# Layers 1 to 3 of the last three pairs batch by batch, turned on TensorE and scaled on VectorE, with closer due dates for the last five pairs

## The chip, the cores and the metric

One core of one Trainium2 chip. The metric is the device time of the whole program in microseconds, as the median of several runs; "span" is the length of the profiled run, some 2 us shorter.

## The reference, cut to what matters

Sixty-four batches of 256 nodes and 128 features pass four layers, each `x = layernorm(x + gnn(x))`. The kernel takes two batches as a pair, so there are 32 pairs (0 to 31), independent of one another.

```
for _ in range(5):                                   # layer 0: five gated steps
    m = adj @ h                                      # used for m_in and m_out
    u3 = h @ u3_w.T + u3_b
    z, r = sigmoid(av @ w3_w.T + w3_b + u3), sigmoid(av @ w4_w.T + w4_b + u3)
    h = (1 - z) * h + z * tanh(av @ w5_w.T + w5_b + (r * h) @ u5_w.T + u5_b)
# layer 1: (A * eye) @ (x W0) + (A * (1 - eye)) @ (x W1) + bias
# layer 2: graph attention (softmax over neighbours), layernorm, relu, GIN, two matmuls
# layer 3: Chebyshev sum over adj, adj^2, adj^3 with seven weight matrices
```

## The kernel before

Every operation is put into a graph with an engine, an estimated cost, and the buffers it touches; a list scheduler then fixes the order on each engine. Among the operations that can start at the same time it takes the lowest rank: the due date of the pair less the longest path from the operation to the pair's end.

```python
def place(p):
    return 20000 * min(p, 28)                        # due date in ns: pairs 28 to 31 are equal
# ...
        for op in reversed(self.ops):
            op.tail = op.cost + max((n.tail + (LATENCY[op.eng] if n.eng != op.eng or op.eng != PE else 0)
                                     for n in op.before), default=0)
        for op in self.ops:
            op.rank = (place(op.rank[0]) - op.tail, op.rank)
```

A "turn" exchanges nodes and features of a tile. VectorE transposes 32x32 blocks, and four DMAs on the SyncE queue put the blocks in place. Layers 1 to 3 have five turns (dT, xT, wT, zT, and xT again), each layer 0 step has one (htok).

```python
        def turn(src, dst, view=lambda b: b.ap, tiles=4):
            S = flat("S") if tiles == 4 else big("S8")
            add(DVE, ..., lambda: nc.vector.transpose(S.ap..., view(src)...), [src], [S], [S])   # cut
            def f():
                for k in range(4):
                    nc.sync.dma_start(dst.ap[:, :, 32 * k:32 * k + 32],
                                      S.ap[32 * k:32 * k + 32].rearrange("s (y r) -> s y r", r=32))
            add(SP, 2730, f, [S], [dst], [dst])
```

The normalisations end with a scaling on ScalarE, in four pieces of 128x128:

```python
                    for c in range(4):
                        nc.scalar.activation(o.ap[:, c, :], view()[:, c, :], AF.Copy, scale=rs.ap[:, c:c + 1])
```

Of the kernel before, what the change touches and what calls it, by code (L numbers as in the profile page):

```python
# [22 lines left out]
N_W = 6  # L23
N_PAIR = 8

MATS = ["w3a", "w3b", "w4a", "w4b", "w5a", "w5b", "u3", "u5",
        "l1w0", "l1w1", "wp", "wpT", "w1", "w2",
        "v0", "v1", "v2", "v3", "v4", "v5", "v6"]
N_L0 = 8
COLS = ["w3_b", "u3_b", "w4_b", "w5_b", "u5_b", "bp", "a_src", "a_dst", "mlp_g", "mlp_b", "e0", "e1"]  # L30
# [8 lines left out]
NORMS = (ACT, ACT, ACT, ACT)  # L39
# [3 lines left out]
def place(p):  # L43

    return 20000 * min(p, 28)
# [111 lines left out]
def kernel(ctx: ExitStack, tc: tile.TileContext, xT, xs, adjs, mats, cols, rows, out):  # L157
# [121 lines left out]
    dg, swap = tall("dg"), tmp([P, P], "swap")  # L279
# [78 lines left out]
    def split():  # L358
        nc.vector.reciprocal(den.ap, den.ap)
        for it in range(2):  # L360
            nc.vector.tensor_scalar(lg.ap[:, it, :], lg.ap[:, it, :], den.ap[:, it:it + 1], None, op0=ALU.mult)
            blk, d = lg.ap[:, it, it * P:(it + 1) * P], dg.ap[:, 0, it * P:(it + 1) * P]
            nc.vector.tensor_mul(d, blk, ident.ap)
            nc.vector.tensor_sub(blk, blk, d)
            nc.vector.tensor_copy(lgs.ap[:, it, :].rearrange("p (t s x) -> p t s x", s=32, x=4),
                                  in_slots(lg.ap[:, it, :]))
        nc.vector.tensor_reduce(dnat.ap, dg.ap[:, 0, :].rearrange("p (t j) -> p t j", j=P), AX.X, ALU.add)
        nc.vector.tensor_copy(swap.ap.rearrange("p (t s x) -> p t s x", s=32, x=4), in_slots(ident.ap))

# [25 lines left out]
    pre(DVE, 2800, split, [ident], [den, lg, dg, lgs, dnat, swap], [dg, lgs, dnat, swap])  # L395
# [75 lines left out]

    t = bank()
# [7 lines left out]

    def build(p):
# [5 lines left out]

        def turn(src, dst, view=lambda b: b.ap, tiles=4):

            S = flat("S") if tiles == 4 else big("S8")  # L490
            add(DVE, 705 if tiles == 4 else 1240,
                lambda: nc.vector.transpose(S.ap.rearrange("p (x c r) -> p x c r", x=4, c=tiles),  # L492
                                            view(src).rearrange("p (c x s) -> p x c s", x=4, c=tiles)),
                [src], [S], [S])

            def f():
                for k in range(4):
                    nc.sync.dma_start(dst.ap[:, :, 32 * k:32 * k + 32],  # L498
                                      S.ap[32 * k:32 * k + 32].rearrange("s (y r) -> s y r", r=32))
            add(SP, 2730, f, [S], [dst], [dst])  # L500
            return dst

        def joined(b):
            return b.ap.rearrange("p t d -> p (t d)")
# [13 lines left out]

        def by_token(terms, consts, also=()):

            t = bank()

            def f():
                for c in range(4):
                    for k, (s, w) in enumerate(terms):
                        nc.tensor.matmul(t.ap[:, c * D:(c + 1) * D], s(c), w,  # L526
                                         start=(k == 0), stop=(k == len(terms) - 1))
            add(PE, 900 * len(terms), f, consts, [t], [t, *also])
            return t

        def full_norm(y):

            st, mv = temp([P, 4, 6], "st", 6), temp([P, 4, 2], "mv", 6)
            rs, nmr = temp([P, 4], "rs", 8), temp([P, 4], "nmr", 6)

            def f():
                for c in range(4):
                    nc.vector.bn_stats(st.ap[:, c, :], y.ap[:, c, :])
                for c in range(4):
                    nc.vector.bn_aggr(mv.ap[:, c, :], st.ap[:, c, :])  # L540
            add(DVE, 1720, f, [y], [st, mv], [st, mv, rs, nmr])

            def f():
                nc.gpsimd.tensor_scalar(rs.ap, mv.ap[:, :, 1], LN_EPS, None, op0=ALU.add)
                nc.gpsimd.tensor_tensor(rs.ap, rs.ap, neg_half.ap, op=ALU.pow)
            add(POOL, 1560, f, [mv, neg_half], [rs])
            add(DVE, 337, lambda: nc.vector.scalar_tensor_tensor(nmr.ap, mv.ap[:, :, 0], -1.0, rs.ap, op0=ALU.mult,
                                                                 op1=ALU.mult), [mv, rs], [nmr])

            def f():  # L550
                for c in range(4):
                    nc.scalar.activation(y.ap[:, c, :], y.ap[:, c, :], AF.Identity, bias=nmr.ap[:, c:c + 1],
                                         scale=rs.ap[:, c:c + 1])
            add(ACT, 1930, f, [nmr, rs], [y])

        def norm(y, view, o, eng, extra=None, takes=()):

            sq, ss, rs = wide("sq"), temp([P, 4], "ss", 6), temp([P, 4], "rs", 8)
            add(ACT, 630, lambda: nc.scalar.activation(sq.ap, view(), AF.Square), [y], [sq], [sq])  # L559

            def f():
                nc.vector.tensor_reduce(ss.ap, sq.ap, AX.X, ALU.add)  # L562
                if extra is not None:
                    nc.vector.scalar_tensor_tensor(ss.ap, ss.ap, 1.0 / D, extra.ap, op0=ALU.mult, op1=ALU.add)  # L564
            add(DVE, 685 if extra is None else 850, f, [sq] + ([] if extra is None else [extra]), [ss], [ss])

            def f():
                if extra is None:
                    nc.gpsimd.tensor_scalar(ss.ap, ss.ap, 1.0 / D, LN_EPS, op0=ALU.mult, op1=ALU.add)  # L569
                nc.gpsimd.tensor_tensor(rs.ap, ss.ap, neg_half.ap, op=ALU.pow)  # L570
            add(POOL, 1400 if extra is None else 1110, f, [ss, neg_half], [ss, rs], [rs])
            if eng == ACT:
                def f():
                    for c in range(4):
                        nc.scalar.activation(o.ap[:, c, :], view()[:, c, :], AF.Copy, scale=rs.ap[:, c:c + 1])
                add(ACT, 1570, f, [y, rs], [o], takes)
            else:
                add(DVE, 700, lambda: nc.vector.tensor_mul(o.ap, view(), rs.ap[:, :, None].to_broadcast([P, 4, D])),
                    [y, rs], [o], takes)
# [6 lines left out]
        for s in range(STEPS):  # L586
# [29 lines left out]
            h = turn(hT, wide("htok"))  # L616
        x_t = h
        add(DVE, 763, lambda: nc.vector.tensor_add(x_t.ap, x_t.ap, x0.ap), [x0], [x_t])
# [5 lines left out]
        def f():  # L624
            for it in range(2):
                o, i = (b.ap.rearrange("p (b t) d -> p b t d", t=2)[:, :, it, :] for b in (xd, x_t))
                nc.scalar.activation(o, i, AF.Copy, scale=dcol.ap[:, it:it + 1])
        add(ACT, 1000, f, [x_t, dcol], [xd], [xd])
        dT = turn(xd, wide("dT"), joined)
        qT = mix(x_t, offT)  # L630
        y = wide("y")
        add(POOL, 1370, lambda: nc.gpsimd.tensor_add(y.ap, x_t.ap, row("l1_bias", 4)), [x_t, rbc], [y], [y])
        t = by_token([(lambda c: qT.ap[:, c * P:(c + 1) * P], mat("l1w1")), (lambda c: dT.ap[:, c, :], mat("l1w0"))],
                     [qT, dT, W1])
        add(DVE, 690, lambda: nc.vector.tensor_add(y.ap, as_tiles(t.ap), y.ap), [t], [y])
        norm(y, lambda: y.ap, y, NORMS[0])
# [3 lines left out]
        xT = turn(x1, wide("xT"), joined)  # L640
        h2 = temp([P, 4, HW], "h2", 6)
        for b in range(2):
            t2 = bank()

            def f(t2=t2, b=b):
                for i in range(2):
                    nc.tensor.matmul(t2.ap[:, i * HW:(i + 1) * HW], xT.ap[:, 2 * b + i, :], wpx.ap,  # L647
                                     start=True, stop=True)
            add(PE, 450, f, [xT, wpx], [t2], [t2] + ([h2] if b == 0 else []))
            add(DVE, 410, lambda t2=t2, b=b: nc.vector.tensor_add(  # L650
                h2.ap[:, 2 * b:2 * b + 2, :], t2.ap[:, :2 * HW].rearrange("p (t d) -> p t d", d=HW),
                hbias.ap[:, None, :].to_broadcast([P, 2, HW])), [t2, hbias], [h2])

        ts, sd = bank(), flat("sd")

        def f():
            for c in range(4):
                nc.tensor.transpose(ts.ap[:, c * P:(c + 1) * P], h2.ap[:, c, D + 1:D + 2].to_broadcast([P, P]), ident.ap)  # L658
        add(PE, 450, f, [h2, ident], [ts], [ts, sd])
        add(ACT, 585, lambda: nc.scalar.copy(sd.ap.rearrange("p (c x s) -> p c x s", x=4, s=32),  # L660
                                             ts.ap.rearrange("p (c s x) -> p c x s", x=4, s=32)), [ts], [sd])
        u = big("u")
        mx, nm, rd = (temp([P, 4], k, 6) for k in ("mx", "nm", "rd"))
# [4 lines left out]
        def f():  # L668
            for c in range(4):
                b, it = divmod(c, 2)  # L670
                nc.vector.tensor_tensor_reduce(
                    out=uc(c), in0=sd.ap[:, b * N:(b + 1) * N], in1=maskb.ap[:, it, :], scale=1.0,
# [4 lines left out]
        add(DVE, 2400, f, [sd, h2, maskb], [u, mx, nm], [u, mx, nm, rd])  # L677

        def f():
            for c in range(4):  # L680
                nc.scalar.activation(uc(c), uc(c), AF.Prelu, bias=h2.ap[:, c, D:D + 1], alpha=SLOPE)
        add(ACT, 2000, f, [h2], [u])

        def f():
            for c in range(4):
                nc.scalar.activation(uc(c), uc(c), AF.Exp, bias=nm.ap[:, c:c + 1], accum_out=rd.ap[:, c:c + 1])
        add(ACT, 2760, f, [nm], [u, rd])
# [124 lines left out]
```

## Time and profile before

| | before |
|---|---|
| median of the first three runs | 1586.88 us (1583.99 to 1587.73) |
| span of the profiled run | 1584.6 us |
| TensorE busy | 1538.7 us, 97% |
| last layer 0 product done | 1462.4 us |
| from there to the end | 122.2 us, with TensorE work of 70.1 |

"TensorE work" here is the number of passes of each width times what a pass takes at full clock, read from start to start where the matmuls are dense: 0.111 us for 128 columns, 0.216 for 256, 0.429 for 512. Over the whole kernel that gives 1515.8 us (some 2 us of it are the few passes of one or two columns in the preparation). Span less work is what is lost: 68.8 us, of which 52.1 (122.2 - 70.1) after the last layer 0 product and 16.7 before it.

### The profile page before, as it was taken

The page shows a single profiled execution, that of the slowest core. Times are in us where ns is not written, and L with a number is a line of the kernel's source. Part 1 is how long each engine was busy: PE and PEld are TensorE (multiplying, and loading weights), DVE is VectorE, ACT ScalarE, POOL GpSimd, SP SyncE. Part 2 cuts the span into 40 slices and gives each one's busy share as a digit, 9 for nine tenths or more (in the row PEclk, how much of TensorE's full clock was granted, in tenths as well). Part 3 has the DMA queues.
Part 4 walks back from the last instruction along what each step waited for, and adds up shares of the span by engine and source line. Part 5 has one row for each costly group of instructions (what it writes and reads, how often), then busy time and mean ns, then how long its engine had stood idle before and what let it go on. Part 6 is the DMA issues. An engine that isn't in the chain of part 4 may idle for free.

```text
span 1584.6 us, 21441 instructions
## 1 busy us (share of the span) xinstructions
PE 1538.7 (97%) x6382; PEld 1070.4 (68%) x6382; DVE 1104.4 (70%) x2465; ACT 992.1 (63%) x2245; POOL 441.5 (28%) x487
## 2 busy tenths in 40 slices
PE   8999999999999999999999999999999999998767
PEld 5556667666677676667676667766767766676656
DVE  4687787667767677767676867776776766677553
ACT  3355676666666666666666666656666666677554
POOL 0001233332222323223323232233232231244441
PEclk9999999999999999999999999999999999999788
DMA  6223444444443444443444444344444344334422
GB/s 204 45 36 52 67 66 84 73 87 84 75 84 74 72 81 87 76 84 74 74 79 87 76 80 79 71 77 87 78 77 85 70 72 88 62 70 68 79 54 60
DMA packets 756611, 121.98 MB, mean 77 GB/s; under 512 B 743184, under 2 KB 743184, under 8 KB 756496
## 3 DMA queue, kind: packets, MB, share of 16 engines
q1 hardware_dynamic: 756208, 120.09, 42.1%
q8 instruction: 52, 0.85, 0.2%
q14 instruction: 63, 0.52, 0.1%
q10 hardware_dynamic: 288, 0.53, 0.1%
HBM read 19.86 MB, written 8.39 MB: 18 GB/s over the span
## 4 chain that ended last, share of the span: by engine, by line
PE 91%; DVE 2%; DMA 2%; ACT 2%; SPq 1%; issue 1%; POOL 1%; POOLq 0%; ACTq 0%; DVEq 0%
PE ps L513 27%; PE ps L607 9%; PE ps L589 9%; PE ps L597 8%; PE ps L605 8%; PE ps L592 8%; PE ps L740 7%; PE ps L526 6%; PE ps L702 4%; PE ps L749 3%; PE ps L647 2%; SPq L498 1%; PE ps L658 1%; DMA wT<-S 1%; DMA hT<-xT_in 1%
## 5 line engine op out<-in xcount | busy, mean ns | idle before, releaser
L516 ACT COPY mix<-ps 128x512 f32<-128x512 f32 x256 | 148.1, 580 | 197.7 <-PE ps L513 196.5
L513 PE MATMUL ps<-aTs,htok 128*128 128x256 f32 x1024 | 242.4, 380 | 2.8 <-DMA htok<-S 2.6
L513 PEld LDWEIGHTS ps<-aTs,htok 128*128 128x128 f32 x1024 | 192.6, 190 | 69.6 <-issue 32.8
L569 POOL TENSOR_SCALAR ss<-ss 128x4 f32<-128x4 f32 x96 | 38.2, 398 | 603.0 <-DVE ss L562 601.7
L611 DVE TENSOR_TENSOR hv<-hv,hT 128x512 f32<-128x512 f32 x160 | 124.2, 777 | 98.8 <-ACT hv L609 97.3
L570 POOL TENSOR_TENSOR rs<-ss,neg_half 128x4 f32<-128x4 f32 x128 | 139.2, 1087 | 192.0 <-DVE ss L564 183.8
L602 DVE SCALAR_TENSOR_TENSOR tr<-tr,hT 128x512 f32<-128x512 f32 x160 | 118.4, 742 | 91.4 <-ACT tr L595 91.3
L607 PE MATMUL ps<-tr,u5h 128*128 128x512 f32 x320 | 163.6, 594 | 0.4 <-DVE tr L602 0.2
L589 PE MATMUL ps<-hT,W 128*128 128x512 f32 x320 | 162.4, 593 | 1.1 <-DMA hT<-xT_in 1.1
L592 PE MATMUL ps<-mix,w4s 128*128 128x512 f32 x320 | 162.9, 593 | 0.0
L597 PE MATMUL ps<-mix,dw 128*128 128x512 f32 x320 | 162.8, 593 | 0.0
L605 PE MATMUL ps<-mix,w5s 128*128 128x512 f32 x320 | 162.6, 593 | 0.0
L609 ACT ACTIVATE hv<-ps,bh 128x512 f32<-128x512 f32 x160 | 109.4, 685 | 83.2 <-PE ps L607 80.6
L600 ACT ACTIVATE tz<-ps,bz 128x512 f32<-128x512 f32 x160 | 109.4, 685 | 60.0 <-PE ps L597 58.6
L595 ACT ACTIVATE tr<-ps,br 128x512 f32<-128x512 f32 x160 | 108.4, 679 | 39.3 <-PE ps L592 39.0
L612 DVE SCALAR_TENSOR_TENSOR hv<-tz,hv 128x512 f32<-128x512 f32 x160 | 108.9, 694 | 24.0 <-ACT tz L600 22.6
L562 DVE TENSOR_REDUCE ss<-sq 128x4 f32<-128x512 f32 x128 | 87.1, 681 | 48.1 <-ACT sq L559 48.1
L492 DVE STREAM_TRANSPOSE S<-hT 128x512 f32<-128x512 f32 x160 | 112.3, 703 | 1.1
L614 DVE SCALAR_TENSOR_TENSOR hT<-hv,hT 128x512 f32<-128x512 f32 x160 | 108.8, 693 | 4.9
L607 PEld LDWEIGHTS ps<-tr,u5h 128*128 128x128 f32 x320 | 60.4, 190 | 50.4 <-issue 36.4
L605 PEld LDWEIGHTS ps<-mix,w5s 128*128 128x128 f32 x320 | 58.6, 191 | 51.5 <-issue 31.1
L589 PEld LDWEIGHTS ps<-hT,W 128*128 128x128 f32 x320 | 58.3, 190 | 49.1 <-issue 42.8
(174 smaller groups left out, 2904.2 us busy)
## 6 DMA issues: line engine op xcount, KB each, us to landing
htok<-S SPq DMA_DIRECT2D x640, 64.0 KB, 2.4
xT<-S SPq DMA_DIRECT2D x256, 64.0 KB, 2.4
wT<-S SPq DMA_DIRECT2D x128, 128.0 KB, 3.8
xs<-xs_in SPq DMA_DIRECT2D x32, 256.0 KB, 2.8
hT<-xT_in SPq DMA_DIRECT2D x32, 256.0 KB, 3.0
dT<-S SPq DMA_DIRECT2D x128, 64.0 KB, 2.3
zT<-S SPq DMA_DIRECT2D x128, 64.0 KB, 2.4
y_out<-o SPq DMA_DIRECT2D x32, 256.0 KB, 2.0
```

The costliest lines, as they stand in the source:

```text
L492: lambda: nc.vector.transpose(S.ap.rearrange("p (x c r) -> p x c r", x=4, c=tiles), view(src).rearrange("p (c x s) -> p x c s", x=4, c=til ...
L513: nc.tensor.matmul(t.ap[:, b * N:(b + 1) * N], src.ap[:, 2 * b + j, :], m.ap[:, j, :], start=(j == 0), stop=(j == 1))
L516: add(ACT, 590, lambda: nc.scalar.copy(o.ap, t.ap), [t], [o])
L570: nc.gpsimd.tensor_tensor(rs.ap, ss.ap, neg_half.ap, op=ALU.pow)
L589: add(PE, 865, lambda tg=tg: nc.tensor.matmul(tg.ap, mat("u3"), hT.ap, start=True, stop=False, skip_group_check=True), [hT, W0], [tg], [tg ...
L592: add(PE, 865, lambda tg=tg, mT=mT: nc.tensor.matmul(tg.ap, w4s.ap, mT.ap, start=False, stop=False, skip_group_check=True), [mT, w4s], [tg])
L597: add(PE, 865, lambda tg=tg, mT=mT: nc.tensor.matmul(tg.ap, dw.ap, mT.ap, start=False, stop=True, skip_group_check=True), [mT, dw], [tg])
L602: add(DVE, 735, lambda tr=tr: nc.vector.scalar_tensor_tensor(tr.ap, tr.ap, 1.0, hT.ap, op0=ALU.add, op1=ALU.mult), [hT], [tr])
L605: add(PE, 865, lambda tv=tv, mT=mT: nc.tensor.matmul(tv.ap, w5s.ap, mT.ap, start=True, stop=False), [mT, w5s], [tv], [tv, hv])
L607: add(PE, 865, lambda tv=tv, tr=tr: nc.tensor.matmul(tv.ap, u5h.ap, tr.ap, start=False, stop=True), [tr, u5h], [tv])
L611: add(DVE, 735, lambda hv=hv: nc.vector.tensor_sub(hv.ap, hv.ap, hT.ap), [hT], [hv])
L740: nc.tensor.matmul(tt[i].ap[:, b * N:(b + 1) * N], s, w.ap.rearrange("p k d -> p (k d)"), start=(b == 0 and k == 0), stop=False, skip_grou ...
```

## The change

The intent is to shorten the end, where TensorE is no longer full. The last three pairs (29 to 31) run layers 1 to 3 as two independent chains of one batch each; in them TensorE transposes through the identity and ScalarE copies the result out of PSUM; VectorE scales; and the due dates of pairs 27 to 31 are 6 us apart in place of 20 us (27 to 28) and none (28 to 31). The five steps of layer 0 stay as they were; the sum and the norm after them already belong to the split chains. Extra copies of some weights in natural order come with it.

```diff
+N_TAIL = 3
 def place(p):
-    return 20000 * min(p, 28)
+    return 20000 * min(p, 27) + 6000 * max(p - 27, 0)
@@ (cut)
+        if p < NPAIR - N_TAIL:
+            layers123(p, add, x_t, x0, (0, 1), False)
+        else:
+            for b in range(2):
+                layers123(p, add, x_t, x0, (b,), True)
+
+    def layers123(p, add, h, x0, bs, by_pe):
+        nb = len(bs)
+        C = 2 * nb
@@ turned(), used for dT, xT, zT and xT of layer 3 (cut)
+            if by_pe:
+                t = bank()
+                def f():
+                    for c in range(C):
+                        nc.tensor.transpose(t.ap[:, c * P:(c + 1) * P], src.ap[:, c, :], ident.ap)
+                add(PE, 112 * C, f, [src, ident], [t], [t, o])
+                ... add(ACT, act(C * P) - 45, lambda: nc.scalar.copy(o.ap, as_tiles(t.ap[:, :C * P])), [t], [o])
+            else:
+                turn(add, src, o, joined)
@@ full_norm (cut)
+            if by_pe:
+                def f():
+                    for c in range(C):
+                        nc.vector.tensor_scalar(y.ap[:, c, :], y.ap[:, c, :], mv.ap[:, c, 0:1], rs.ap[:, c:c + 1],
+                                                op0=ALU.subtract, op1=ALU.mult)
+                add(DVE, 350 * C, f, [mv, rs, nmr], [y])
+                return
@@ norm (cut)
+            if by_pe:
+                add(DVE, dve(C * D), lambda: nc.vector.tensor_mul(o.ap, view(), rs.ap[:, :, None].to_broadcast([P, C, D])),
+                    [y, rs], [o])
+                return
@@ the same for wT; the rest takes C and nb for 4 and 2, and the swapped weights (cut)
```

## The prediction

> **What bounds the kernel now.** I read the page's engine rows and its 40 slices first (is one engine full, and where is it not), then windows over the two halves that differ, then the order of matmuls and TensorE's waits in the part that is not full.
>
> ```profile
> span 1584.6 us, 21441 instructions
> ...
> PE 1538.7 (97%) x6382; PEld 1070.4 (68%) x6382; DVE 1104.4 (70%) x2465; ACT 992.1 (63%) x2245; POOL 441.5 (28%) x487
> ...
> PE   8999999999999999999999999999999999998767
> ...
> PEclk9999999999999999999999999999999999999788
> ```
>
> TensorE is full in 35 slices. The first slice loses 6 us to loads; the last four (some 40 us each) have both idle time and a lower granted clock. So nothing that saves work on another engine helps before about 1420 us.
>
> ```profile
> 400.00:800.00 400.00, 400.00 (x1685) 279.38 (x1684) 289.20 (x642) 260.31 (x595) 115.94 (x128) 1.00 0.44 78
> 1390.00:1430.00 40.00, 40.00 (x197) 30.57 (x195) 30.89 (x86) 30.81 (x74) 19.07 (x21) 1.00 0.39 68
> 1430.00:1463.00 33.00, 29.62 (x151) 22.35 (x150) 24.41 (x61) 22.88 (x59) 11.63 (x15) 1.00 0.48 75
> ...
> 1463.00:1585.00 122.00, 86.69 (x404) 73.85 (x404) 60.00 (x155) 68.43 (x183) 44.46 (x55) 0.84 0.35 63
> ```
>
> Columns: window, length, busy PE, PEld, DVE, ACT, POOL with counts, granted clock, DMA share, GB/s. I cut at 1463 because the timeline has the last layer 0 matmul there; what follows is layers 1 to 3 alone:
>
> ```profile
> 1461.52 1.02 PE L607 MATMUL ps<-tr,u5h 128*128 128x512 f32 x2
> 1462.38 0.60 PE L658 MATMUL ps<-ident,h 128*128 128x128 f32 x4
> 1469.48 3.78 PE L513 MATMUL ps<-aTss,hb 128*128 128x256 f32 x8 [6.50 <-ACT hb L552]
> ```
>
> Full-speed matmul costs, from start to start in the dense timeline: a 512-column product (two passes) 0.86 us, eight 256-column passes 1.73 us, eight 128-column passes 0.89 us. A pair's layer 0 step is 1.73 + 5 x 0.86 = 6.0, five steps 30.2; its layers 1 to 3 are 17.0; together 47.2, times 32 = 1511, plus about 6 of preparation: 1517 us of TensorE work. After 1463 the counts by form are 232 passes of 256 columns and 172 of 128: 232 x 0.216 + 172 x 0.111 = 69 us. In 122 us, then, 53 are lost: 122 - 86.7 = 35 idle, and 86.7 - 69 = 18 to the clock. That is all there is to win, beside some 8 us between 1414 and 1463 and at the start.
>
> What TensorE waits for in that window:
>
> ```profile
> PE ps L513 <- ACT hb L552: 8.6, 2, 6.5
> PE ps L702 <- DMA wT<-S: 7.1, 2, 3.8
> PE ps L513 <- ACT hg L711: 3.7, 1, 3.7
> PE ps L526 <- ACT zT L719: 3.4, 2, 2.0
> PE ps L740 <- DMA xT<-S: 3.2, 2, 2.8
> ```
>
> No single wait dominates: normalisation on ScalarE and GpSimd, and the DMA turns. It is the length of the chain of one pair. The last pair's layers 1 to 3 take from 1463 to the end, 120 us, and four pairs due at the same time (the place function is capped at pair 28) run in lockstep. One turn by DMA in the timeline:
>
> ```profile
> 1520.18 1.25 DVE L492 STREAM_TRANSPOSE S<-u 128x1024 f32<-128x1024 f32 x1
> ...
> 1521.45 3.66 SPq L498 DMA_DIRECT2D wT<-S  x4
> ...
> 1525.21 8.78 SPq L498 DMA_DIRECT2D zT<-S  x12
> ...
> 1527.92 3.33 PE L702 MATMUL ps<-h,wT 128*128 128x128 f32 x16 [3.22 <-DMA wT<-S]
> ```
>
> 7.7 us from the transpose's start to the matmul; and twelve issues for three zT in a row take 8.8 us of one queue, so pairs in lockstep also queue for SyncE.
>
> **What the Trainium skill says.** "TensorE: Matmul & The Clock Gate", Part 4 (PE-mode transpose): a transpose is a matmul against the identity, about 275 ns in a kernel, its result in PSUM, so a copy follows. The trace agrees: the four transposes of L658 last 272 ns each but advance in 0.44 us together, 0.11 each.
>
> ```profile
> 1416.37 0.60 PE L658 MATMUL ps<-ident,h 128*128 128x128 f32 x4
> 1416.81 1.02 PE L597 MATMUL ps<-mix,dw 128*128 128x512 f32 x2
> ```
>
> The same page, Part 1: TensorE falls to half clock after an idle window of about 3.4 us. The trace agrees: after the 6.5 us gap above, the eight passes took 3.6 us to the next group, not 1.73. So a closed gap pays about twice. "DMA: Bandwidth & Descriptors", Anatomy of one DMA: about 2 us of a DMA are fixed, mostly the receipt of the write (its figure is for the GpSimd path). Here, on the SP queue, 64 KB took 2.4 us and 128 KB 3.8, so halving a turn's size alone would have gained little. "SBUF — State Buffer", two separate sides: VectorE with two SBUF inputs and GpSimd lock each other out. In this tail the two-input L725 took 842 ns on average, over the whole kernel 715: it agrees, and the change gives VectorE more of such work.
>
> **The change part by part.** Pairs 29 to 31 become six chains of one batch each.
>
> Removed per such pair: five turns (VectorE 4 x 0.70 + 1.22 = 4.0 us, 20 DMA issues at about 0.65 us, and on the chain four latencies of about 5 us and one of 7.7); on ScalarE the four norm scalings (y, z, o, hg: 4 x 4 x 0.39 = 6.2 us less on the hg, read from PSUM, 0.37), the two full ones (8 x 0.41 = 3.3 us) and the copy sd (0.58).
>
> Added: 24 transposes a pair x 0.11 = 2.7 us of TensorE, 8 us for three pairs. Their copies on ScalarE: an estimate of 0.39 for 256 columns and 0.58 for 512 (from R's 0.37 and mix's 0.58); per batch dT, xT, xT3 and wT make 3 x 0.39 + 0.58 = 1.75, 3.5 us a pair (zT's activation was there before). Scaling on VectorE: 4 x 0.41 per batch (L753's size), and four 128x128 scalings at 0.29 (L411).
>
> VectorE per batch, halves of the measured operations: about 10.7 us (adds and multiplies of 256 columns 0.41 each x 13, statistics 0.6 twice, scores 1.3, u 0.7, the rest small), 21.4 a pair against 18.3 now. ScalarE 9.0 a batch, GpSimd about 7.6 (its pow with two columns instead of four is guessed at 0.65, from 1.01 at four). TensorE 17.0 / 2 + 1.35 = 9.9.
>
> Chain of one batch in layers 1 to 3: I added the same operations in order: today about 92 us for a pair by measured lengths (with the five turns 28), plus 5 of semaphores; the run shows 120 with queueing. For a batch: full norms 2 x 2.7, four norms 9, scores to weights 5.5, turns 5 x 0.7, GpSimd affine 1.5, matmuls 7, copies and adds 8, output 3, semaphores 5: near 48 us.
>
> Due dates: pairs 27 to 31 are now due 6 us apart, where 28 to 31 were equal. With a 48 us chain behind layer 0, the last layer 0 ends with pair 29 some 12 us and pair 30 some 6 us into their layers, and 27 and 28 near their ends: TensorE work left 5 + 7 + 15 + 17 + 20 = 64 us, VectorE 64, ScalarE about 55, GpSimd about 45. No longer the chain (48) but two engines at 64 bound this phase. I take 85% use and a drain of about 5 us: 80 us where 122 are now.
>
> Sum: TensorE work 1517 + 8 + 0.5 = 1525.5, of which 64 lie in the last phase; 1461.5 before it + 6 start + 9 lost on the way = 1476.5; + 80 = 1556.5 of span; the timed run is 2.3 above the span (1586.88 against 1584.6): 1559, rounded to 1560. So 53 us of loss become about 16, 8 are paid back in transposes: 27 us, 1.7%.
>
> **The rivals.** First, VectorE becomes the bound of the last phase: six chains that each need VectorE for 10.7 of 48 us ask for 134% of it, and GpSimd locks its two-input operations. For it: the L725 row; against it: today it is 60 of 122 us busy there. At 75% use the phase takes 90 us: 1570. Second, the chain stays: each small operation has a fixed part (a 256-column copy 0.37, a 512 one 0.58), so half a batch is not half the time, and the last pair's two batches end alone at half clock. The phase would take 95 us: 1575. Third, the closer due dates leave the last layer 0 starved: five pairs in lockstep on one SP queue, as L513 waited for htok twice (2.6 us) in 1414 to 1463 already; 5 to 10 us: 1565 to 1570. Fourth, the better way: the scheduler fills the phase to 95% with little clock loss: 70 us, 1549. The larger weight load (1.2 MB for 0.8) and the extra weight preparation lie in stages where TensorE is full, and should cost nothing.
>
> **Range and chances.** The first three move it up by 5 to 15 us, the fourth down by 10. Predicted 1560 us, range 1545 to 1577. Faster by over 2% needs at most 1555: the phase must be 75 us or less; 0.33. Within 2%: 0.64. Slower: 0.03, only if the schedule of the last pairs falls apart.
>
> **What would show it.** Right: TensorE still full to about 1430; last layer 0 matmul near 1475; from there to the end about 80 us at a mean clock above 0.9; no wait on wT or xT by DMA in it; 72 more transposes at 0.11. Wrong: VectorE over 90% in that phase (first rival); gaps of over 3 us with all engines half idle (second); waits on htok before 1475 (third); or a slice below 9 before 1400 us, which would mean that the steady state changed.

## The result, and the profile after

| | before | after |
|---|---|---|
| median, runs beside each other | 1587.31 us | 1565.52 us (1564.42 to 1567.36) |
| ratio | | 0.9868 (0.9851 to 0.9885) |
| span | 1584.6 | 1564.1 |
| TensorE work | 1515.8 | 1524.2 |
| last layer 0 product done | 1462.4 | 1461.1 |
| lost before it | 16.7 | 14.0 |
| lost after it | 52.1 | 25.9 |

A ratio is the mean time of one kernel's fast runs over that of the other's in the same rounds, so not quite the ratio of the medians. It is a gain of 1.3%: clear of noise, below 2%. All outputs are right.

The page of the changed kernel: its span, the engines' busy times, and the 40 slices of TensorE and of its granted clock.

```profile
span 1564.1 us, 21663 instructions
...
PE 1538.2 (98%) x6480; PEld 1072.5 (69%) x6480; DVE 1100.4 (70%) x2550; ACT 992.3 (63%) x2227; POOL 459.5 (29%) x532
...
PE   8999999999999999999999999999999999999797
...
PEclk9999999999999999999999999999999999999998
```

The digits that were 8767 are now 9797, and the clock stays up but for the last slice. Nothing else has moved: the windows of the full stretch are alike (400 to 800 us: TensorE 400.00 busy in both). Windows of the end, cut at the last layer 0 product (length, then busy time of PE, PEld, DVE, ACT, POOL with counts; then clock, DMA share, GB/s):

```profile
1414.00:1461.00 47.00, 46.57 (x198) 32.96 (x197) 30.78 (x67) 27.78 (x61) 18.20 (x22) 1.00 0.47 71
1461.00:1564.00 103.00, 85.11 (x509) 75.30 (x507) 73.48 (x240) 57.29 (x164) 56.27 (x94) 0.92 0.12 27
1461.00:1484.00 23.00, 14.88 (x99) 13.16 (x98) 20.78 (x74) 15.59 (x47) 12.69 (x22) 0.97 0.19 35
1484.00:1558.00 74.00, 70.05 (x412) 62.13 (x410) 50.68 (x162) 41.01 (x118) 41.77 (x69) 0.92 0.09 22
```

The end phase is 103 us where it was 122, although 7 us more TensorE work is left in it. It has two faces. In its first 23 us VectorE is busy 20.8 and TensorE only 14.9; in the next 74, TensorE is nearly full. TensorE's waits in this phase (who waited for whom, us in total, times, longest):

```profile
PE ps L630 <- DVE x_t L667: 6.6, 2, 5.4
PE ps L630 <- ACT hg L818: 2.9, 1, 2.9
PE ps L643 <- ACT zT L826: 0.9, 1, 0.9
PE ps L611 <- DVE y L699: 0.6, 1, 0.6
```

No DMA is left in the list, where wT and xT cost 10 us before. The list has three more waits, all for ScalarE and of 0.5 us or less. The longest wait is now for a VectorE scaling (L667, the end of the norm after layer 0). In the timeline (start, length, engine, line, what, idle before and its cause):

```profile
1477.25 0.60 PE L751 MATMUL ps<-ident,h 128*128 128x128 f32 x4
...
1478.06 0.71 POOL L662 TENSOR_TENSOR rs<-rs,neg_half 128x2 f32<-128x2 f32 x1
...
1482.80 1.11 DVE L667 TENSOR_SCALAR x_t<-x_t,mv,rs 128x128 f32<-128x128 f32 x4
...
1483.29 3.75 PE L630 MATMUL ps<-offT,x_t 128*128 128x256 f32 x8 [5.44 <-DVE x_t L667]
...
1528.19 2.08 PE L630 MATMUL ps<-ginT,hg 128*128 128x256 f32 x4 [2.92 <-ACT hg L818]
```

The first gap is a matter of VectorE's queue: GpSimd had the scale factors of the pair's first batch at 1478.77 (1478.06 + 0.71), but VectorE, busy throughout, came to the scaling at 1482.80, after 4 us of other work; the factors of the second batch were there only at 1482.05. Each gap is paid twice: after it the same eight passes take 3.75 us, not 1.89, and the windows from 1483 to 1487 show a granted clock of 0.50.

### The profile page after: what moved, and what is told of

Same layout as the page of the kernel before. It is cut to its first block, busy times and chain, and to the rows that moved or that the text cites. A ratio compares the mean times of both kernels' runs of the same rounds, so it can differ in the third digit from the quotient of the medians.

```text
span 1564.1 us, 21663 instructions
## 1 busy us (share of the span) xinstructions
PE 1538.2 (98%) x6480; PEld 1072.5 (69%) x6480; DVE 1100.4 (70%) x2550; ACT 992.3 (63%) x2227; POOL 459.5 (29%) x532
## 4 chain that ended last, share of the span: by engine, by line
PE 94%; DVE 2%; POOL 1%; DMA 1%; SPq 1%; issue 0%; ACT 0%; POOLq 0%; DVEq 0%
PE ps L533 17%; PE ps L630 10%; PE ps L547 9%; PE ps L565 8%; PE ps L550 8%; PE ps L555 8%; PE ps L563 8%; PE ps L643 7%; PE ps L858 7%; PE ps L809 4%; PE ps L870 3%; PE ps L741 2%; PE ps L751 1%; SPq L514 1%; POOL rs L695 0%
## 5 line engine op out<-in xcount | busy, mean ns | idle before, releaser
L569 DVE TENSOR_TENSOR hv<-hv,hT 128x512 f32<-128x512 f32 x160 | 111.1, 695 | 134.2 <-ACT hv L567 132.3
L694 POOL TENSOR_SCALAR ss<-ss 128x4 f32<-128x4 f32 (+1 forms) x105 | 31.8, 303 | 513.0 <-DVE ss L686 498.7
L536 ACT COPY mix<-ps 128x512 f32<-128x512 f32 x160 | 94.0, 587 | 131.7 <-PE ps L533 131.7
L695 POOL TENSOR_TENSOR rs<-ss,neg_half 128x4 f32<-128x4 f32 (+1 forms) x140 | 137.7, 984 | 91.3 <-DVE ss L688 78.7
L560 DVE SCALAR_TENSOR_TENSOR tr<-tr,hT 128x512 f32<-128x512 f32 x160 | 111.0, 695 | 64.1 <-ACT tr L553 63.1
L661 POOL TENSOR_SCALAR rs<-mv 128x4 f32<-128x4 f32 (+1 forms) x70 | 34.9, 499 | 282.1 <-DVE mv L657 279.6
L572 DVE SCALAR_TENSOR_TENSOR hT<-hv,hT 128x512 f32<-128x512 f32 x160 | 112.8, 707 | 4.3 <-PE ps L858 0.5
L686 DVE TENSOR_REDUCE ss<-sq 128x4 f32<-128x512 f32 (+1 forms) x140 | 87.8, 633 | 25.0 <-ACT sq L683 24.8
L633 ACT COPY mix<-ps 128x512 f32<-128x512 f32 (+1 forms) x105 | 57.6, 549 | 71.1 <-PE ps L630 71.1
L743 DVE TENSOR_TENSOR h<-ps,hbias 128x260 f32<-128x260 f32 x64 | 27.2, 426 | 102.0 <-PE ps L741 101.9
```

Of the source, the lines that this page charges most:

```text
L560: add(DVE, 735, lambda tr=tr: nc.vector.scalar_tensor_tensor(tr.ap, tr.ap, 1.0, hT.ap, op0=ALU.add, op1=ALU.mult), [hT], [tr])
L569: add(DVE, 735, lambda hv=hv: nc.vector.tensor_sub(hv.ap, hv.ap, hT.ap), [hT], [hv])
L572: add(DVE, 735, lambda hv=hv: nc.vector.scalar_tensor_tensor(hT.ap, hv.ap, 0.5, hT.ap, op0=ALU.mult, op1=ALU.add), [hv], [hT])
L695: nc.gpsimd.tensor_tensor(rs.ap, ss.ap, neg_half.ap[:, :C], op=ALU.pow)
```

## The experiments

All use the changed kernel with one thing altered; the runs of the unchanged kernel before stand beside each. In the table at the end of this section "lost" is span less TensorE work.

**The due dates alone.**

```diff
-N_TAIL = 3
+N_TAIL = 0
```

> The changed kernel with no tail pairs: only the five close due dates are left (times given for medians of before 1587, changed 1565.5). Chain theory (the end phase is as long as one pair's chain through layers 1 to 3, and the change wins by shortening that chain): nothing shortens a chain here, so 1582 to 1592. Due-date theory (the order of work at the end is what wins): 1562 to 1570.

Measured: 1604.01 us against 1586.74, ratio 1.0106 (1.0089 to 1.0122): slower than before, beyond both theories. With due dates spread and long chains, the last pair ends alone. Its last 32 us (window), and the matmuls in it (timeline):

```profile
1571.00:1603.00 32.00, 13.99 (x40) 10.44 (x40) 4.95 (x15) 6.25 (x15) 2.46 (x4) 0.61 0.13 29
```

```profile
1573.81 2.08 PE L643 MATMUL ps<-W,zT 128*128 128x128 f32 x8 [7.78 <-ACT zT L826]
1580.81 3.78 PE L630 MATMUL ps<-aTss,hb 128*128 128x256 f32 x8 [4.93 <-ACT hb L676]
1587.36 1.19 PE L858 MATMUL ps<-vx,xT 128*128 128x256 f32 x2 [2.77 <-DMA xT<-S]
```

Three waits in a row with no other TensorE work to fill them, and a mean clock of 0.61.

**The three tail pairs alone, with the old due dates.**

```diff
-    return 20000 * min(p, 27) + 6000 * max(p - 27, 0)
+    return 20000 * min(p, 28)
```

> The changed kernel with the old due dates (20 us apart, capped at pair 28) and the three tail pairs as changed. Chain theory: most of the gain stays, 1567 to 1573. Due-date theory: the gain is gone, 1582 or more. If the two only work together (short chains need layer 0 of the last pairs to end together with enough other work left), this run and the due dates alone are both near or above 1585.

Measured: 1595.39 us against 1586.74, ratio 1.0049 (1.0029 to 1.0070). The chains are the short ones, and the gain is gone. The chain theory, which is that of the prediction, falls here; what holds is the last sentence of the expectation. TensorE before the last layer 0 product, from the timeline:

```profile
1444.19 2.41 PE L533 MATMUL ps<-aTs,htok 128*128 128x256 f32 x8 [3.92 <-DMA htok<-S]
...
1460.23 2.74 PE L565 MATMUL ps<-tr,u5h 128*128 128x512 f32 x6
1462.80 2.74 PE L555 MATMUL ps<-mix,dw 128*128 128x512 f32 x6
```

The counts x6 are three pairs doing the same product one after the other: layer 0 of three pairs in lockstep, by the code the tail pairs, waiting for its turn by DMA with little else ready. In the changed kernel the same lines come as x2 with other work between, and the last three layer 0s end at 1440, 1449 and 1461. By the table below lockstep before the last layer 0 product is the smaller part of what this run loses against the changed kernel, 12.3 us; 17.6 are lost after it, in waits for hg, u and hb (6.8, 5.3 and 4.4 us), as all six chains start within a few us of each other. The rank rule fits this: a shorter chain to the end makes a pair's layer 0 less urgent, so with the old dates the tail pairs' layer 0 falls behind that of pair 28 and is left over; that part of the reason is read from the code.

**The split with DMA turns.** The six chains keep their split, their VectorE scaling and the new due dates; only the turns go back to VectorE and DMAs, at half size, and with them a ScalarE copy (sd) that their order of nodes needs.

```diff
-                layers123(p, add, x_t, x0, (b,), True)
+                layers123(p, add, x_t, x0, (b,), False)      # scaling on VectorE kept by a flag of its own
@@ turn()
-        S = flat("S") if tiles == 4 else big("S8")
+        S = flat("S") if tiles == 4 else (big("S8") if tiles == 8 else temp([P, 256], "t", N_T, "S"))
```

> Last three pairs batch by batch and scaled on VectorE, due dates as changed, but every turn in layers 1 to 3 again through VectorE's 32x32 transposes and DMAs (half size, so twice as many). If the DMA turns were the part of the chain that counts: 1575 to 1585, with TensorE waiting for wT and xT by DMA in the end phase. If the split alone did it: 1563 to 1568 (it saves 8 us of TensorE transposes).

Measured: 1585.84 us, ratio 0.9993 (0.9978 to 1.0008): no gain at all, a little past the upper end of the expectation. A stretch of the SyncE queue in the end phase (a half turn of xT has pieces of 32 KB, one of wT 64 KB), and TensorE's waits for DMAs in that phase:

```profile
1511.22 8.48 SPq L514 DMA_DIRECT2D wT<-S  x12
1519.79 2.65 SPq L514 DMA_DIRECT2D xT<-S  x4
1522.54 2.65 SPq L514 DMA_DIRECT2D wT<-S  x4
```

```profile
PE ps L860 <- DMA xT<-S: 4.4, 3, 2.1
PE ps L645 <- DMA dT<-S: 3.5, 3, 2.6
PE ps L743 <- DMA xT<-S: 3.3, 2, 1.9
PE ps L811 <- DMA wT<-S: 2.8, 2, 1.8
```

TensorE waits 14.0 us for turns there, as the expectation had it, and 5.2 us once shortly before; with TensorE turns it waits for none in that phase. The queue does not rest from 1511 to 1525. Four issues take 2.65 us for 32 KB pieces as for 64 KB ones, so two half turns take twice the queue of a whole one of 64 KB pieces. And a 32 KB piece lands in 2.0 us where 64 KB takes 2.5. Here splitting without taking the turns off the queue bought nothing. One rival is left in: the transposes for the turns also load VectorE, which is busy 90.8 us of this end phase against 73.5, so not all of the 20 us need be the DMAs.

**TensorE turns without the split.** Both batches of a pair together, all else as changed.

```diff
-            for b in range(2):
-                layers123(p, add, x_t, x0, (b,), True)
+            layers123(p, add, x_t, x0, (0, 1), True)          # wT in two banks
```

> Last three pairs with TensorE transposes and VectorE scaling, but both batches of a pair together. If the split into two independent half chains counts: 1572 to 1582, with more idle TensorE in the end phase and a longer drain (about 1.5 us more after the last matmul). If only the turns count: 1563 to 1568.

Measured: 1574.87 us against 1586.74, ratio 0.9923 (0.9908 to 0.9939). Giving up the split costs 9 us against the changed kernel, and giving up the TensorE turns cost 20 in the run before; together that is more than the gain of 22, so the two work in part on the same loss. This run loses 20.2 us before the last layer 0 product, where the changed kernel loses 14.0, and 25.5 after it, nearly the same 25.9. So neither the longer drain nor more idle TensorE at the end, which the expectation named, decides it. (The profiled execution was the fastest of its four, 3 us below the median.)

**Scaling back on ScalarE.**

```diff
+        by_dve = False
@@ full_norm and norm
-            if by_pe:
+            if by_dve:
```

> The changed kernel with the scalings of the six tail chains back on ScalarE (128x128 pieces with a per-partition scale, as before). If VectorE bounds the end phase (it is busy 73 of 103 us there and 20.8 of the first 23), freeing it helps: 1558 to 1564. If the length of the chain counts (a 128x256 scaling is 0.42 us on VectorE against 2 x 0.39 on ScalarE, and a full norm's 2 x 0.29 against 0.34 and 2 x 0.49): 1570 to 1578.

Measured: 1563.08 us, ratio 0.9849 (0.9832 to 0.9865). The intervals of this and of the changed kernel overlap, so both were run again in the same five rounds, together with two tail pairs.

> The changed kernel as it is, again, beside the three below on the same chip: 1564 to 1567.

> Three tail pairs, scaling on ScalarE, again. If VectorE's load holds up the start of the end phase (TensorE waited 5.4 us for a VectorE scaling there, with ScalarE scaling 2.6): 2 to 4 us below the changed kernel of the same rounds. If the earlier 2 us were noise between chips: within 1 us of it.

Measured: the changed kernel 1565.76 us (1564.02 to 1566.18), ratio 0.9863; with ScalarE scaling 1561.93 us (1560.77 to 1563.04), ratio 0.9841. The runs of the two do not overlap: with three tail pairs, moving the scaling to VectorE costs about 4 us. The end phase with ScalarE scaling, from the same cut, and TensorE's longest wait in it:

```profile
1457.00:1559.00 102.00, 87.62 (x526) 76.13 (x524) 57.68 (x208) 80.69 (x240) 54.84 (x98) 0.95 0.14 30
```

```profile
PE ps L632 <- ACT x_t L678: 2.6, 1, 2.6
```

VectorE is busy 58 us of it in place of 73, the wait for the norm after layer 0 is 2.6 us where it was 6.6, and 21.8 us are lost after the last layer 0 product, not 25.9.

**Two tail pairs, with either scaling.**

```diff
-N_TAIL = 3
+N_TAIL = 2
```

> Two tail pairs instead of three, scaling on VectorE. If a tail pair is worth only what its chain saves at the very end, two are enough and save 24 transposes (2.7 us): 1561 to 1565. If three short chains are needed to fill the end phase: 1568 to 1574.

> Two tail pairs and scaling on ScalarE. If both effects are real and add up: 2 to 4 us below two tail pairs with VectorE scaling; the fastest of the four, 1558 to 1563, if two tail pairs are enough.

Measured: 1563.84 us with VectorE scaling (ratio 0.9851), 1565.86 with ScalarE scaling (ratio 0.9865). Two tail pairs are enough, as the first expectation had it, but the two effects do not add: with two pairs ScalarE scaling is 2 us slower, with three 4 us faster. With two pairs and ScalarE scaling, ScalarE is busy 68.1 of the last 96.5 us (50.9 of 87 with VectorE scaling) and TensorE's longest wait, 3.1 us, is for a ScalarE scaling. But every variant gets another order from the scheduler, and differences of 2 to 4 us should be read with that in mind.

**Eight tail pairs.**

```diff
-N_TAIL = 3
+N_TAIL = 8
```

> Eight tail pairs instead of three. Each further pair adds 24 transposes at 0.11 us to a stretch where TensorE is full. If a TensorE transpose costs its full 0.11 us there: 5 x 2.66 = 13 us slower than the changed kernel, 1577 to 1581. If the shorter chains of the further pairs also pay: 1566 or less.

Measured: 1580.89 us, ratio 0.9960. The 120 further transposes add 13.6 us of TensorE work (1537.8 against 1524.2), and the span grows by 15.1. That fits the full 0.11 us for a TensorE transpose in a full stretch; the run does not isolate it, since the split and the scaling of those five pairs change with it.

**Which part of the due dates.** First the spread without the earlier start, then the earlier start without the spread.

```diff
-    return 20000 * min(p, 27) + 6000 * max(p - 27, 0)
+    return 20000 * min(p, 28) + 6000 * max(p - 28, 0)     # spread only
+    return 20000 * min(p, 27)                             # equal dates from pair 27 on
```

> Due dates 6 us apart from pair 28 on (so the last pair is due at 578 instead of 564, counted as in the changed kernel's function), all else as changed. If it is the spread among the three tail pairs that counts (they must not run in lockstep): 1565 to 1572. If it is that they are due earlier against the pairs before them: 1580 or more.

> Pairs 27 to 31 all due at the same time as pair 27: earlier than in the old due dates, but with no spread. If the spread counts: 1580 to 1590. If only earliness counts: 1563 to 1568.

Measured: spread only 1572.95 us (ratio 0.9913), equal dates 1581.97 (ratio 0.9967), both 1565.5. The first is 1 us above its expectation, the second inside it. The spread does more, and the earlier dates help too: neither alone is the cause. It is not that the last layer 0 ends earlier: with equal dates its last product is done at 1457.9, with the spread alone at 1475.0.

The account of all this, in us. Each row is one profiled execution, which lies up to 3.2 us from the median of its kernel:

| kernel | span | TensorE work | lost before the last layer 0 product | lost after it |
|---|---|---|---|---|
| before | 1584.6 | 1515.8 | 16.7 | 52.1 |
| changed | 1564.1 | 1524.2 | 14.0 | 25.9 |
| due dates alone | 1603.2 | 1516.0 | 30.5 | 56.7 |
| tail pairs alone | 1593.9 | 1524.2 | 26.3 | 43.5 |
| split, DMA turns | 1582.5 | 1516.1 | 23.7 | 42.7 |
| TensorE turns, no split | 1569.7 | 1524.0 | 20.2 | 25.5 |
| equal dates | 1578.2 | 1524.2 | 22.1 | 32.0 |
| spread only | 1572.7 | 1524.2 | 20.1 | 28.4 |
| two tail pairs | 1561.7 | 1521.5 | 20.2 | 20.0 |
| two tail pairs, ScalarE scaling | 1565.1 | 1521.5 | 18.1 | 25.5 |
| ScalarE scaling, second run | 1559.0 | 1524.2 | 13.0 | 21.8 |

The last row is the fastest kernel; its median of 1561.93 us is below the kernel before and the changed one.

## Why the prediction was right or wrong

The time was right: 1560 predicted, 1565.5 measured, inside the range, and within 2% as held most likely. The reasons were right in part, and to that extent the number was luck: the chain theory, which is the prediction's, gave 1567 to 1573 for the tail pairs with the old due dates, and that run took 1595.

- **Where the loss lies.** Right. TensorE stays full to 1461 us, the steady part did not move, and nearly all of the gain is in the end: 26.2 us less lost after the last layer 0 product, 2.7 before it, 8.4 paid back in transposes; 20.5 of span.
- **The price of the transposes.** Predicted 8 us, and 8.4 by the passes counted in the traces (1524.2 - 1515.8); the run with eight tail pairs fits it (13.6 counted, 15.1 of span).
- **The turns by DMA.** Right that they are a costly part of the chain, and right that halving them would gain little: with half turns by DMA TensorE waited 14.0 us for them and the gain vanished.
- **The due dates.** This step failed. It had pair 29 "some 12 us" and pair 30 "some 6 us into their layers" at the end of the last layer 0, hence 64 us of TensorE work left and the last layer 0 product near 1475. It was done at 1461, and 77 us were left. The group row shows that none of the three tail pairs had begun layer 1: its first product has 24 passes still to come, eight for each of them. What the step left out is the way from a pair's last layer 0 product to its first layer 1 product (gates, turn, sum, norm), in which the pair gives TensorE nothing. In the timeline of TensorE the last three layer 0s end at 1440.4, 1449.0 and 1461.1, and the three first products start at 1461.1, 1471.0 and 1483.3: 21 to 22 us each, if the pairs keep their order, longer than the 12 and 6 us that the pairs were ahead.

```profile
L630 PE MATMUL ps<-offT,x_t 128*128 128x256 f32 x24 | 7.6, 472 | 6.6 <-DVE x_t L667 6.6
```

- **The use of the end phase.** Taken were 85% and a drain of 5 us (64 / 0.85 + 5 = 80); measured were 77 us of work in the 97.1 up to the last matmul, 79%, and a drain of 5.9, between the prediction and the 75% of its first rival. The phase lost 25.9 us instead of 16; the rest of the sum held (14.0 lost before it, against 15), which is the whole of the error: 10 - 1 - 1.3 of TensorE work = some 7.6 us of span.
- **The rival VectorE.** Partly right. VectorE is busy 71% of the phase, not over 90%, but 90% of its first 23 us, where the longest wait is for it; with three tail pairs taking the scaling off it gained 4 us, with two it lost 2. The prediction had counted this load (21.4 us a pair against 18.3), but no loss from it in its central figure.
- **The cause.** The prediction put the gain down to the shorter chain and treated the dates as a mere input of the work left. Each half alone made the kernel slower, by 1.1% and 0.5%. The shorter chains cost 0.5% with the old dates, where the last layer 0s end together, and gained 0.3% with equal dates from pair 27, 0.9% with the spread alone and 1.3% with both; the new dates without short chains left a long chain to run alone at the end. This interaction was not among the rivals. The third rival (layer 0 in lockstep on one SyncE queue) described what happens, but put it on the new dates; it is the old dates with short chains that showed it.
- **Small terms.** A pow with two columns on GpSimd took 0.72 to 0.75 us, guessed 0.65. Of the 24 VectorE scalings of 256 columns in the end phase 21 took the 0.41 to 0.43 that was assumed and three 0.94 or 0.95. These three have two SBUF inputs and run beside a GpSimd operation of 256 columns; with its data in PSUM (hg) the same multiplication took 0.42 beside such an operation (L815, 1500.89 to 1501.61). That agrees with the lock between VectorE and GpSimd that the "SBUF — State Buffer" page names (section "Who interferes with whom"). The 128x128 scalings advanced in 0.28 to 0.30 us each, as assumed; only one group of four took 1.51 us.

```profile
1472.80 1.59 POOL L725 TENSOR_TENSOR y<-x_t,rbc 128x256 f32<-128x256 f32 x2
...
1472.86 0.94 DVE L699 TENSOR_TENSOR y<-y,rs 128x256 f32<-128x256 f32 x1 [0.87 <-POOL rs L695]
...
1500.95 0.42 DVE L699 TENSOR_TENSOR hg<-ps,rs 128x256 f32<-128x256 f32 x1 [0.24 <-POOL rs L695]
```

What stays open: why ScalarE scaling gains with three tail pairs and loses with two; and how much of each difference is the chance of another order, which no run measures: every variant is one order of the scheduler, and the 8 us that the tail pairs alone lost are not free of it. The idle time at the start of the phase could not be shown to be VectorE's alone, since moving the scaling also moved the order.

## What to carry to other kernels

When the bound engine runs dry at the end, look at what is left there and in what order it ends: here shorter chains and the order of the last items had to be changed together, and a test of each alone showed a loss although both together won. Move latency off a shared queue before splitting work into smaller pieces, if a piece takes as long to issue as the whole (2.65 us for a turn of 32 or 64 KB pieces). Pay for latency with the full engine's time only where that engine is not full.

## What the Trainium skill lacked or had wrong

- "TensorE: Matmul & The Clock Gate", Part 1: it gives an idle window of about 3.4 us for the fall to half clock. Here a gap of 2.92 us was followed by four passes in 2.08 us, twice the 1.03 of the same four passes at 1523 us in the same trace. In windows of 1 us the granted clock is 0.93 from 1526 and 0.50 from 1527, so the fall came some 1.6 us after the last matmul had ended at 1525.27; in the gap of 5.44 us it came some 4.6 us after (estimates from the windows).
- The same page, Part 4: it gives the duration of a transpose (about 275 ns; 272 here) but not the rate, which is what a full TensorE pays: four fp32 transposes advanced in 0.44 us, and in the run with 120 further ones, 13.6 us by this rate, the span grew by 15.1.
- "DMA: Bandwidth & Descriptors", Anatomy of one DMA: its fit of 2.0 us plus bytes over 436 GB/s is for the GpSimd path. On the SyncE queue with packets of under 512 B, 32, 64 and 128 KB took 2.0, 2.4 to 2.5 and 3.7 to 3.8 us; and its 50 ns of dispatch are for that path too: on the SyncE queue four issues took 2.65 us, 0.66 each, for pieces of 32 and 64 KB.
- No page has the time of a pow on GpSimd: by the means of the groups 128x4 took 1.03 to 1.19 us, 128x2 0.71 to 0.75.
